# A graph layer's message loop on one core: additions, clipping and bf16 splitting moved into PSUM, two groups at a time

## The chip, the cores and the metric

The kernel runs on one core of one Trainium2 chip. Times are device microseconds of one execution, lower is better. A time shown for a kernel is the median over several executions. The engines are PE (TensorE: matmuls, with PEld for its weight loads), DVE (VectorE), ACT (ScalarE), POOL (GpSimd) and SP (SyncE, which here only issues DMAs). Each works through its own instructions in order and waits on semaphores that others raise.

## The reference

A graph layer with 12500 nodes of 96 features and 412500 edges, which are sorted by their target node. In short:

```python
node_feat = mlp(x, W_node, ...)
edge_feat = mlp(edge_attr, W_edge, ...)          # 4 -> 96
message = concatenate([x[row], x[col], edge_feat], axis=1)
message = mlp(message, W_msg, ...)               # 288 -> 96
agg = segment_sum(message, col, num_segments=N)
x = layernorm(x + agg + node_feat)
```

Here `mlp` is `relu(h @ W + b)`, followed by a normalization of each feature over all rows (all nodes, or all edges). A message's value before its `relu` is therefore the sum of a row of `x @ W_msg[:96]` picked by `row`, a row of `x @ W_msg[96:192]` picked by `col`, and a product of the edge's features. The normalization needs each feature's sum and sum of squares over all edges.

## The kernel before

**Ahead of the loop.** The kernel writes `p_tab` and `q_tab` (the two products of `x`) to HBM, computes the node part and the edge features' statistics (`edge_norm`, L306 to L312), and gathers the rows of `p_tab` for the first 104 groups of edges into HBM (`spill`), through `stage` tiles. A gather (L175) is one indirect DMA, which POOL issues for 128 edges; it fetches 128 rows of 96 floats.

**Groups and blocks.** 128 edges are a tile, 4 tiles a group (`GT`), 4 groups a block (`BG`). There are 806 groups in 202 blocks. 26 blocks ("early") take their rows from `spill` by one DMA into `pb` (L440); the other 176 ("late", 702 groups) take them from tiles `pg`, which POOL fills by four gathers a group, into a ring of `RING` = 21 tiles. The first 21 are gathered ahead of the loop. After that, the gathers of group g + 21 are issued once the addition of group g has read its tile. Early blocks stand among the late ones, about one to seven. The first three early blocks (`RAW`) hold rows of `x` and not of `p_tab`; `convert` multiplies them.

**One step** of the message loop (L568) is one group, k. Its instructions are put in order by hand (`manual_schedule`), so each engine takes them in the order of the source:

- `edges` (L462): PE multiplies the edge features of the next block, all four groups, into `pr`, four banks of PSUM. `prepare` (L469): ACT clips the four into `left`, one instruction of 2048 columns, two steps later.
- `linear` (L475): PE multiplies `left` by `rhs` for group k + 1, four products into one of two banks `z`. `rhs` holds the weights and the 31 rows of `q_tab` that the block's targets lie in; the columns of `left` behind the edge features pick among them.
- `message` (L483): DVE adds `z` (PSUM) and `pg` (SBUF) into `hs` (SBUF). The third one of a block also builds `at`, the 0/1 matrix of edges by target nodes.
- `first_part` (L498), once a block: ACT clips `hs`, copies it to bf16 (`h`, part 0), and squares it into `sq`. `second_part` (L507), a step later: DVE subtracts part 0 from `hs`, ACT copies the rest to bf16 (part 1), DVE sums the squares (L514) and adds them to `squares`. `third_part` (L520): DVE subtracts part 1 and writes part 2. Three bf16 parts carry the fp32 value. These instructions take 1536 columns each.
- `sums` (L525): PE multiplies `at` by the three parts and adds up in `pa`, `LATER` = 6 steps behind. `fold`, `turn` and `add` bring a block's sums into `agg`.

In the last block the three parts are run group by group.

**Order and queues.** SP issues the loads of block s + 2 (`load`, `fetch`) at the start of block s. POOL issues nothing in the loop but gathers.

Of the kernel before, what the change touches and what calls it, by code (L numbers as in the profile page):

```python
# [11 lines left out]
F32 = mybir.dt.float32  # L12
# [41 lines left out]
RING = 21  # L54
RAW = 3
LATER = 6
# [20 lines left out]
def gnn(ctx, tc, t):  # L77
# [265 lines left out]
    def fast(ring):  # L343
# [35 lines left out]
        with tc.tile_pool(name="fix", bufs=1) as fix, tc.tile_pool(name="msg", bufs=2) as work, \  # L379
# [28 lines left out]
            zb = [ps.tile([P, GE], F32, name=f"z{i}", bufs=1) for i in range(2)]  # L408
            nodes_of = zb[0][:, GT * C:GT * C + BG * WN].rearrange("p (k w) -> p k w", w=WN)
            nc.vector.tensor_copy(nodes_of, iota)  # L410

            eas, block, prs, zs, pas, hss, by_node = {}, {}, {}, {}, {}, {}, {}
# [31 lines left out]
            def convert(s):  # L444

                b = order[s]
                px = ps.tile([P, BG, GE], F32, name="pr", bufs=1)
                for i in range(0, BG, 2):
                    for k in range(2 * GT):
                        nc.tensor.transpose(px[:C, k // GT, k % GT * P:(k % GT + 1) * P],  # L450
                                            got[b * BG + i + k // GT][:, k % GT, :], ident)
                    for h in range(2):
                        xt = work.tile([P, BG, GT, C], F32, name="sq", bufs=1)
                        xt = xt.rearrange("p g t c -> p (g t c)")[:C, :GE]
                        nc.scalar.activation(xt, px[:C, h, :], AF.Copy)
                        for k in range(GT):
                            nc.tensor.matmul(px[:, 2 + h, k * C:(k + 1) * C], xt[:, k * P:(k + 1) * P], w_msg[:, 0, :],
                                             start=True, stop=True)
                        nc.vector.tensor_copy(got[b * BG + i + h],
                                              px[:, 2 + h, :GT * C].rearrange("p (k c) -> p k c", c=C))  # L460

            def edges(s):  # L462

                prs[s] = ps.tile([P, BG, GE], F32, name="pr", bufs=1)
                for i in range(min(BG, NG - order[s] * BG)):
                    nc.tensor.matmul(prs[s][:C + WN, i, :], we[Q * i:Q * i + EK + 2, :],  # L466
                                     block[s][Q * i:Q * i + EK + 2, :], start=True, stop=True)

            def prepare(s):  # L469

                n = min(BG, NG - order[s] * BG)
                pr, x = prs[s], left[s % 2]
                nc.scalar.activation(x[:C + WN, :n, :], pr[:C + WN, :n, :], AF.Relu)  # L473

            def linear(k):  # L475
                s, g = steps[k]
                n = min(GT, NT - g * GT)
                zs[k] = zb[k % 2][:, :GT * C].rearrange("p (t c) -> p t c", c=C)
                for i in range(n):
                    nc.tensor.matmul(zs[k][:, i, :], left[s % 2][:KR, g % BG, i * P:(i + 1) * P],  # L480
                                     rhs[:KR, s % RB, g % BG, :], start=True, stop=True)

            def message(k):  # L483
# [3 lines left out]
                z, pg = zs.pop(k), got.pop(g)  # L487
                if i == 0:
                    hss[s] = work.tile([P, BG, GT, C], F32, name="hs")
                nc.vector.tensor_add(hss[s][:, i, :n, :], z[:, :n, :], pg[:, :n, :])  # L490
# [7 lines left out]
            def first_part(s, lo, hi, n):  # L498

                hs, h = hss[s][:, lo:hi, :n, :], hb[s % HB][:, lo:hi, :n, 0, :C]  # L500
                nc.scalar.activation(hs, hs, AF.Relu)  # L501
                nc.scalar.activation(h, hs, AF.Copy)  # L502
                sq = work.tile([P, BG, GT, C], F32, name="sq", bufs=1)
                nc.scalar.activation(sq[:, :hi - lo, :n, :], hs, AF.Square)  # L504
                return sq

            def second_part(s, lo, hi, n, sq, rows=P):  # L507

                hs, h = hss[s][:, lo:hi, :n, :], hb[s % HB][:, lo:hi, :n, :, :]
                nc.vector.tensor_tensor(hs, hs, h[:, :, :, 0, :C], op=OP.subtract)  # L510
                nc.scalar.activation(h[:, :, :, 1, :C], hs, AF.Copy)  # L511
                sum_of = work.tile([P, C], F32, name="sum_of", bufs=1)
                m = n if rows == P else n - 1
                nc.vector.tensor_reduce(sum_of, sq[:, :hi - lo, :m, :].rearrange("p g t c -> p c g t"),  # L514
                                        axis=AX.XY, op=OP.add)
                nc.vector.tensor_add(squares, sum_of, squares)
                if rows < P:
                    nc.vector.tensor_add(squares[:rows], sq[:rows, 0, m, :], squares[:rows])

            def third_part(s, lo, hi, n):  # L520

                hs, h = hss[s][:, lo:hi, :n, :], hb[s % HB][:, lo:hi, :n, :, :]
                nc.vector.tensor_tensor(h[:, :, :, 2, :C], hs, h[:, :, :, 1, :C], op=OP.subtract)  # L523
# [15 lines left out]
            def fold(s):  # L539
                by_node[s] = work.tile([NW, C + 1], F32, name="by_node", bufs=1)  # L540
# [18 lines left out]
            with tc.manual_schedule(engines={ET.SP, ET.Pool, ET.PE, ET.DVE, ET.Activation}):  # L559
# [4 lines left out]
                edges(0)  # L564
                prepare(0)
                linear(0)
                held = {}
                for k in range(len(order) * BG + LATER + 3):  # L568
                    s, g = steps[min(k, n - 1)]
                    whole = s < len(order) - 1  # L570
# [4 lines left out]
                    if k % BG == 1 and k // BG - 1 in held:  # L575
                        del held[k // BG - 1]
                        third_part(k // BG - 1, 0, BG, GT)
                    if k + 1 < n:
                        linear(k + 1)
                    if k < n and g % BG == 3 and s + 1 < len(order) and order[s + 1] < RAW:  # L580
                        convert(s + 1)
                    if k < n:
                        message(k)
                        i, m = g % BG, min(GT, NT - g * GT)
                        if whole and i == BG - 1:
                            held[s] = first_part(s, 0, BG, GT)
                        if i == 0 and s:
                            second_part(s - 1, 0, BG, GT, held[s - 1])
                        if not whole:
                            sq = first_part(s, i, i + 1, m)  # L590
                            second_part(s, i, i + 1, m, sq, min(P, E - (g * GT + m - 1) * P))
                            third_part(s, i, i + 1, m)
                    if k % BG == 2 and 0 <= (k - 10) // BG:
                        fold((k - 10) // BG)
                    if k % BG == 3 and 0 <= (k - 11) // BG:
                        turn((k - 11) // BG)
# [7 lines left out]
                    if k % BG == 0 and 0 <= (k - 12) // BG:  # L604
                        add((k - 12) // BG)
# [243 lines left out]
```

## Time and profile before

| | |
|---|---|
| median of 3 runs | 5155.51 us (5140.26 to 5171.73) |
| the profiled execution | 5138.11 us |
| its span, first to last instruction | 5136.4 us |
| mean granted clock of PE | 0.623 |
| busy: PE, PEld | 2712.5 us (53%), 2042.3 us (40%) |
| busy: DVE, ACT | 2464.7 us (48%), 1912.1 us (37%) |
| busy: POOL | 3475.1 us (68%) |

In a row of groups, "x702 | 379.8, 554 | 1427.8" means 702 instructions, 379.8 us in which one of them ran, 554 ns for one on average, and 1427.8 us in which their engine stood idle just before them; what ended that idle time follows the arrows. "remote" means that a semaphore ended it whose writer the profile can't name, "issue" that no wait is seen. In a row of a time line stand the start and the length in us, then engine, line, operation and tiles, with the idle time before it in brackets. The loop runs from 949 us to 5091 us of the span.

### The profile page before, as it was taken

Reading aid. Unit: us, or ns where it says so; the run is one execution under the profiler, and the core shown is the slowest. Engines: PE = TensorE matmul, PEld = TensorE weight load, DVE = VectorE, ACT = ScalarE, POOL = GpSimd, SP = SyncE. Lnnn points to the kernel's source line nnn. Section 1 sums busy time; section 2 is a strip of 40 time slices with the busy share of each in tenths; the row PEclk is TensorE's granted clock in tenths of the full one; section 3 lists DMA queues with packets and bytes.
Section 4 is the critical chain, followed back from the end, with each engine's and each line's share of the span. In section 5 each row is a group of like instructions: output and inputs, shape, how many; then the busy total and the mean of one; then the engine's idle time right before and its main releaser. Section 6 shows DMA issues by size and latency. Waiting matters only on the chain. (4 is left out here: it accounts for less than half of the span.)

```text
span 5136.4 us, 41113 instructions
## 1 busy us (share of the span) xinstructions
PE 2712.5 (53%) x13498; PEld 2042.3 (40%) x13498; DVE 2464.7 (48%) x3234; ACT 1912.1 (37%) x1413; POOL 3475.1 (68%) x3244
## 2 busy tenths in 40 slices
PE   5566753446455656436546363566446635454465
PEld 3423421344334435325434252455325424343354
DVE  2555753445344546425455362566236525454465
ACT  2244542234234435324334252355224414343343
POOL 6645354276577777767777777777767767777771
PEclk7555555566566657656666575677557656666666
DMA  8433332121122212112112222122212212111222
GB/s 233 118 66 73 72 69 41 25 46 42 29 45 47 46 38 54 41 42 46 44 38 48 44 47 48 37 46 48 47 43 45 47 36 47 43 44 39 45 47 80
DMA packets 190356, 273.95 MB, mean 53 GB/s; under 512 B 121571, under 2 KB 121956, under 8 KB 189126
## 3 DMA queue, kind: packets, MB, share of 16 engines
q0 software_dynamic: 103136, 158.62, 15.4%
q1 hardware_dynamic: 71684, 99.14, 7.0%
q10 hardware_dynamic: 15312, 13.47, 0.9%
q8 instruction: 109, 1.79, 0.2%
q14 instruction: 115, 0.94, 0.1%
HBM read 227.55 MB, written 43.43 MB: 53 GB/s over the span
## 5 line engine op out<-in xcount | busy, mean ns | idle before, releaser
L175 POOL DMA_INDIRECT pg<-p_tab,src x2807 | 3056.7, 1089 | 1210.8 <-issue 785.1
L480 PE MATMUL z<-rhs,left 128*128 128x96 f32 x6446 | 1301.9, 368 | 1737.9 <-DVE hs L490 988.9
L480 PEld LDWEIGHTS z<-rhs,left 128*128 128x128 f32 x6446 | 1205.2, 277 | 2040.9 <-DVE hs L490 1067.3
L490 DVE TENSOR_TENSOR hs<-z,pg 128x384 f32<-128x384 f32 x702 | 379.8, 554 | 1427.8 <-remote 870.7
L535 PE MATMUL pa<-h,at 128*80 128x291 bf16 x3223 | 759.0, 367 | 153.4 <-issue 143.4
L473 ACT ACTIVATE left<-pr 127x2048 f32<-127x2048 f32 x202 | 377.6, 1869 | 911.5 <-remote 825.2
L501 ACT ACTIVATE hs<-hs 128x1536 f32<-128x1536 f32 x203 | 298.9, 1473 | 910.8 <-DVE hs L490 630.2
L175 POOL DMA_INDIRECT stage<-p_tab,src x368 | 354.0, 962 | 321.0 <-DMA spill<-stage 197.6
L514 DVE TENSOR_REDUCE sum_of<-sq 128x96 f32<-128x1536 f32 x203 | 558.6, 2752 | 0.0
L306 PE MATMUL pr<-ea,wide 10*128 10x512 f32 x1212 | 407.6, 1074 | 272.6 <-issue 155.3
L535 PEld LDWEIGHTS <-at 128*80 128x80 bf16 x3223 | 461.3, 153 | 225.0 <-issue 178.3
L511 ACT ACTIVATE h<-hs 128x1536 bf16<-128x1536 f32 x203 | 301.6, 1486 | 656.2 <-DVE hs L510 442.4
L312 DVE BATCH_NORM_STATS2 estats<-r 128x6 f32<-128x512 f32 x606 | 365.9, 678 | 309.2 <-issue 181.1
L510 DVE TENSOR_TENSOR hs<-hs,h 128x1536 f32<-128x1536 f32 x203 | 354.3, 1745 | 305.0 <-issue 201.5
L310 ACT ACTIVATE r<-pr 128x1024 f32<-128x1024 f32 x303 | 295.1, 1024 | 447.7 <-remote 272.0
L306 PEld LDWEIGHTS pr<-ea,wide 10*128 10x128 f32 x1212 | 202.7, 322 | 476.2 <-issue 280.2
L523 DVE TENSOR_TENSOR h<-hs,h 128x1536 bf16<-128x1536 f32 (+1 forms) x203 | 353.0, 1739 | 0.0
L502 ACT ACTIVATE h<-hs 128x1536 bf16<-128x1536 f32 x203 | 302.1, 1488 | 6.5
L504 ACT ACTIVATE sq<-hs 128x1536 f32<-128x1536 f32 x203 | 294.7, 1452 | 0.2 <-DVE sum_of L514 0.2
L466 PE MATMUL pr<-ea,we 7*127 7x512 f32 x1404 | 237.5, 691 | 32.6 <-issue 20.0
L490 DVE TENSOR_TENSOR hs<-z,pb 128x384 f32<-128x384 f32 x104 | 56.5, 554 | 233.6 <-remote 174.3
L494 DVE TENSOR_TENSOR at<-rel,z 128x496 bf16<-128x496 f32 x202 | 134.4, 665 | 63.8 <-remote 44.2
(127 smaller groups left out, 1052.0 us busy)
## 6 DMA issues: line engine op xcount, KB each, us to landing
pg<-p_tab,src POOLq DMA_INDIRECT x2807
spill<-stage SPq DMA_DIRECT2D x26, 768.0 KB
pb<-spill SPq DMA_DIRECT2D x26, 768.0 KB
ea<-in_ea SPq DMA_DIRECT2D x75, 160.0 KB
rhs<-q_tab SPq DMA_DIRECT2D x202, 46.5 KB
ea<-in_ea SPq DMA_DIRECT2D x352, 20.0 KB
stage<-p_tab,src POOLq DMA_INDIRECT x368
y_d<-y0s SPq DMA_DIRECT2D x12, 384.0 KB
```

The lines of the kernel that those rows point to most:

```text
L175: nc.gpsimd.indirect_dma_start(out=pg[:, i, :], out_offset=None, in_=tab[:, :], in_offset=bass.IndirectOffsetOnAxis(ap=idx[:, k:k + 1], ax ...
L306: nc.tensor.matmul(pr[:, k % 2, :], wide[Q * i:Q * i + 2 * EK, :], ea[Q * i:Q * i + 2 * EK, b % J, :], start=True, stop=True)
L312: nc.vector.bn_stats(stats[:, (k - o) % NS, (k - o) // NS, :], r[:, 1 - o, :])
L473: nc.scalar.activation(x[:C + WN, :n, :], pr[:C + WN, :n, :], AF.Relu)
L480: nc.tensor.matmul(zs[k][:, i, :], left[s % 2][:KR, g % BG, i * P:(i + 1) * P], rhs[:KR, s % RB, g % BG, :], start=True, stop=True)
L490: nc.vector.tensor_add(hss[s][:, i, :n, :], z[:, :n, :], pg[:, :n, :])
L502: nc.scalar.activation(h, hs, AF.Copy)
L510: nc.vector.tensor_tensor(hs, hs, h[:, :, :, 0, :C], op=OP.subtract)
L511: nc.scalar.activation(h[:, :, :, 1, :C], hs, AF.Copy)
L514: nc.vector.tensor_reduce(sum_of, sq[:, :hi - lo, :m, :].rearrange("p g t c -> p c g t"), axis=AX.XY, op=OP.add)
L523: nc.vector.tensor_tensor(h[:, :, :, 2, :C], hs, h[:, :, :, 1, :C], op=OP.subtract)
L535: nc.tensor.matmul(pas[s][:NW, :3 * (C + 1)], at[s % HB][:r, i, o + NW * t:o + NW * (t + 1)], h[:r, t, :, :].rearrange("p a c -> p (a c)") ...
```

## The change

The values of a group no longer go to `hs`. DVE adds `pg` to the product where it lies, in PSUM, and clipping, subtracting and splitting work there too. For that `z` becomes two buffers of two banks, each for a pair of groups. The three parts run for each pair, with instructions of 768 columns, and a buffer comes free for the products of the pair after next when the third part has read it. `pr` shrinks from four banks to two, so that `edges` and `prepare` run twice a block, for half of it each. `convert` goes group by group. The space of `hs` and of a smaller `sq` makes a ring of 26 tiles possible. `sums` run 4 steps behind; `fold`, `turn` and `add` follow one step after another.

```diff
-RING = 21
+RING = 26
-LATER = 6
+LATER = 4
...
-            zb = [ps.tile([P, GE], F32, name=f"z{i}", bufs=1) for i in range(2)]
+            zb = [ps.tile([P, 2, GE], F32, name=f"z{i}", bufs=1) for i in range(2)]
...
-            def edges(s):
-
-                prs[s] = ps.tile([P, BG, GE], F32, name="pr", bufs=1)
-                for i in range(min(BG, NG - order[s] * BG)):
-                    nc.tensor.matmul(prs[s][:C + WN, i, :], we[Q * i:Q * i + EK + 2, :],
-                                     block[s][Q * i:Q * i + EK + 2, :], start=True, stop=True)
...
+            def edges(s, half):
+
+                n = min(2, NG - order[s] * BG - 2 * half)
+                if n > 0:
+                    prs[s, half] = ps.tile([P, 2, GE], F32, name="pr", bufs=1)
+                for i in range(n):
+                    o = Q * (2 * half + i)
+                    nc.tensor.matmul(prs[s, half][:C + WN, i, :], we[o:o + EK + 2, :], block[s][o:o + EK + 2, :],
+                                     start=True, stop=True)
...
+                    nc.scalar.activation(x[:C + WN, 2 * half:2 * half + n, :], pr[:C + WN, :n, :], AF.Relu)
...
-                if i == 0:
-                    hss[s] = work.tile([P, BG, GT, C], F32, name="hs")
-                nc.vector.tensor_add(hss[s][:, i, :n, :], z[:, :n, :], pg[:, :n, :])
+                z = zb[k // 2 % 2][:, k % 2, :n * C].rearrange("p (t c) -> p t c", c=C)
+                nc.vector.tensor_add(z, z, got.pop(g)[:, :n, :])
...
+            def parts(k, m, n):
+
+                s, g = steps[k]
+                z = zb[k // 2 % 2][:, k % 2:k % 2 + m, :n * C].rearrange("p g (t c) -> p g t c", c=C)
+                return z, [hb[s % HB][:, g % BG:g % BG + m, :n, a, :C] for a in range(3)]
+
+            def first_part(k, m=2, n=GT):
+
+                z, h = parts(k, m, n)
+                nc.scalar.activation(z, z, AF.Relu)
+                nc.scalar.activation(h[0], z, AF.Copy)
+                sq = work.tile([P, 2, GT, C], F32, name="sq")
+                nc.scalar.activation(sq[:, :m, :n, :], z, AF.Square)
+                return sq
...
+            def second_part(k, sq, m=2, n=GT, rows=P):
+
+                z, h = parts(k, m, n)
+                nc.vector.tensor_tensor(z, z, h[0], op=OP.subtract)
+                nc.scalar.activation(h[1], z, AF.Copy)
+                sum_of = work.tile([P, C], F32, name="sum_of")
...
+            def third_part(k, m=2, n=GT):
+
+                z, h = parts(k, m, n)
+                nc.vector.tensor_tensor(h[2], z, h[1], op=OP.subtract)
...
+                    if k % 2 and 3 <= k <= last + 1:
+                        third_part(k - 3)
                     if k + 1 < n:
                         linear(k + 1)
                     if k < n:
                         message(k)
...
+                    if k % 2 == 0 and 2 <= k <= last:
+                        second_part(k - 2, sq)
+                    if k % 2 and k < last:
+                        sq = first_part(k - 1)
...
                     if 0 <= k - LATER < n:
                         sums(k - LATER)
                     if k < n and s + 1 < len(order):
-                        if g % BG == 0:
-                            edges(s + 1)
-                        if g % BG == 2:
-                            prepare(s + 1)
+                        (prepare if g % 2 else edges)(s + 1, g % BG // 2)
+                        if g % BG == 3 and order[s + 1] < RAW:
+                            convert(s + 1)
```

More of the change, by code (lines that the diff above doesn't have):

```diff
@@ L446, in convert @@
                 b = order[s]
[L447 to L460, printed above, removed]
@@ L462, in edges @@
[L462 to L473 removed]
+                px = ps.tile([P, 2, GE], F32, name="pr", bufs=1)
@@ L563, in fast @@
                 fetch(1)
-                edges(0)
-                prepare(0)
+                for half in range(2):
+                    edges(0, half)
+                    prepare(0, half)
                 linear(0)
-                held = {}
+                sq, last = None, BG * (len(order) - 1)
                 for k in range(len(order) * BG + LATER + 3):
                     s, g = steps[min(k, n - 1)]
-                    whole = s < len(order) - 1
                     if k < n and g % BG == 0:
```

76 lines of the change are left out of this document (33 added, 43 removed).

## The prediction

> **What bounds the kernel now.** I read the groups first, then the waits, then time lines and windows. The page's chain of waits covers only the last 45 us, so the message loop has to be read from the other views. Gathers are POOL's `DMA_INDIRECT` (L175); 2807 of them feed the loop. From the groups by line:
>
> ```profile
> span 5136.4 us, 41113 instructions
> ...
> L175 POOL DMA_INDIRECT pg<-p_tab,src x2807 | 3056.7, 1089 | 1210.8 <-issue 785.1 <-DVE hs L490 379.6 <-DMA pg<-p_tab,src 44.5
> ...
> L514 DVE TENSOR_REDUCE sum_of<-sq 128x96 f32<-128x1536 f32 x203 | 558.6, 2752 | 0.0
> ...
> L490 DVE TENSOR_TENSOR hs<-z,pg 128x384 f32<-128x384 f32 x702 | 379.8, 554 | 1427.8 <-remote 870.7 <-PE z L480 267.7 <-DMA pg<-p_tab,src 117.3
> L473 ACT ACTIVATE left<-pr 127x2048 f32<-127x2048 f32 x202 | 377.6, 1869 | 911.5 <-remote 825.2 <-issue 35.9 <-PE pr L466 23.2
> ...
> L310 ACT ACTIVATE r<-pr 128x1024 f32<-128x1024 f32 x303 | 295.1, 1024 | 447.7 <-remote 272.0 <-issue 114.8 <-PE pr L306 44.8
> ```
>
> POOL's account of these gathers is 3056.7 + 1210.8 = 4267.5 us, about the whole time from its first one (748 us) to its last (5016 us). The reader is to see that DVE's adds hardly wait for gathered rows (117 us), and that 871 us end with "remote", a releaser that the profile can't name. The time lines show what stretches a gather:
>
> ```profile
> 2999.74 1.76 DVE L510 TENSOR_TENSOR hs<-hs,h 128x1536 f32<-128x1536 f32 x1 [2.31 <-ACT sq L504]
> ...
> 3000.78 1.53 POOL L175 DMA_INDIRECT pg<-p_tab,src  x1 [0.30 <-issue]
> ...
> 3004.96 1.75 DVE L523 TENSOR_TENSOR h<-hs,h 128x1536 bf16<-128x1536 f32 x1
> 3005.11 2.41 POOL L175 DMA_INDIRECT pg<-p_tab,src  x1 [0.30 <-issue]
> ...
> 3009.08 0.95 POOL L175 DMA_INDIRECT pg<-p_tab,src  x1 [0.30 <-issue]
> 3009.29 0.56 DVE L490 TENSOR_TENSOR hs<-z,pg 128x384 f32<-128x384 f32 x1 [0.70 <-PE z L480]
> ...
> 3010.33 0.94 POOL L175 DMA_INDIRECT pg<-p_tab,src  x1 [0.30 <-issue]
> ...
> 3014.29 1.76 DVE L510 TENSOR_TENSOR hs<-hs,h 128x1536 f32<-128x1536 f32 x1 [1.81 <-issue]
> ```
>
> A gather takes 0.94 us and one starts every 1.25 us. One that begins inside L523 (both inputs in SBUF) is held until L523 ends, 2.41 us in all; one inside L490 (one input in PSUM) isn't. So (1089 - 944) x 2807 = 407 us of POOL is time held by DVE. A block takes 14.55 us here (2999.74 to 3014.29), while 16 gathers need 20 us. DVE eats faster than POOL supplies, yet the gathers aren't what it waits for. The windows of the edge statistics, ahead of the loop, where DVE has no such operation, tell why:
>
> ```profile
> 728.40:739.40 11.00, 11.00 (x41) 7.78 (x37) 11.00 (x20) 7.90 (x8) 8.50 (x9) 0.50 0.57 104
> 739.40:853.00 113.60, 25.99 (x51) 6.03 (x48) 16.45 (x26) 12.28 (x12) 85.85 (x91) 0.50 0.26 56
> 853.00:867.00 14.00, 2.08 (x4) 0.50 (x4) 1.29 (x2) 1.44 (x2) 0.00 (x0) 0.50 0.02 4
> 867.00:881.00 14.00, 13.29 (x42) 6.99 (x45) 12.52 (x21) 11.53 (x13) 0.00 (x0) 0.50 0.25 36
> ```
>
> The columns after the length are busy time and count of PE, PEld, DVE, ACT and POOL. POOL gathers from 728.45 to 852.97 without a pause. PE keeps its pace for 11 us (41 matmuls), then does 51 in 113.6 us, 0.45 per us, and is back only 15 us after POOL has stopped. The granted clock is 0.50 in all four rows, so it isn't the clock. A shorter run of 19.7 us shows the same with a shorter return:
>
> ```profile
> 709.28 0.94 POOL L175 DMA_INDIRECT stage<-p_tab,src  x1 [0.30 <-issue]
> ...
> 712.80 8.04 PE L306 MATMUL pr<-ea,wide 10*128 10x512 f32 x24 [2.13 <-ACT r L310]
> ...
> 867.66 12.86 PE L306 MATMUL pr<-ea,wide 10*128 10x512 f32 x39 [5.62 <-ACT r L310]
> ```
>
> PE returns 2.6 us after that run (690.57 to 710.22) and 14.7 us after the one of 124.5 us: 12 to 13% of the run. I read it as a backlog that unbroken gathers build up and only a pause drains. What passes between the engines I can't name. In the loop L510 and L523 hold POOL for 0.6 + 1.5 us in 14.55 us, 14%, which is just enough. When a block comes late, they come too rarely, and it tips over:
>
> ```profile
> 2993.00:3022.00 29.00, 18.55 (x115) 15.41 (x115) 19.24 (x25) 15.78 (x11) 22.93 (x20) 0.74 0.19 38
> 2129.00:2245.00 116.00, 24.93 (x83) 16.27 (x84) 19.46 (x24) 11.47 (x8) 79.47 (x81) 0.50 0.17 34
> ...
> 2132.86 0.56 DVE L490 TENSOR_TENSOR hs<-z,pg 128x384 f32<-128x384 f32 x1 [9.59 <-remote]
> ...
> 2233.86 0.56 DVE L490 TENSOR_TENSOR hs<-z,pg 128x384 f32<-128x384 f32 x1 [7.93 <-remote]
> ```
>
> 57 matmuls make a block; 115 in 29 us are two blocks, 83 in 116 us one and a half, and one block's adds take from 2132.86 to 2233.86, 101 us, with POOL gathering at its full pace. It ends when the ring is full and POOL has to wait for an add:
>
> ```profile
> POOL pg L175 <- DVE hs L490: 379.6, 87, 100.9
> ...
> 852.02 0.95 POOL L175 DMA_INDIRECT pg<-p_tab,src  x1 [0.31 <-issue]
> 953.86 0.94 POOL L175 DMA_INDIRECT pg<-p_tab,src  x1 [100.89 <-DVE hs L490]
> ...
> 5091.14 0.14 issue
> ```
>
> So the loop is set by POOL's pace plus the pauses that PE needs. The row of waits is us, times, longest.
>
> **The change part by part.**
>
> Add, subtract and split in PSUM: L510 and L523 lose an SBUF input. 407 us of held gathers go; the only DVE operation with two SBUF inputs left is the 0.26 us add into `squares`, which I cost at nothing since a gather of 3009.08's kind rarely meets it. With that go the two forced breathing spaces per block. No row shows DVE writing PSUM; 0.55 us (L490, PSUM in) is the nearest, bounded by 2752/4 = 0.69 us per 384 columns (L514) and 1.75/4 = 0.44 (L523). Even 0.69 adds 0.14 x 4 = 0.6 us a block, under POOL's 20.
>
> Pairs instead of fours, half blocks for edges: ACT's 1024 columns take 1.024 and 2048 take 1.869, so each extra instruction costs 0.18 us; five more a block are 0.9 us on ACT, and three more big ones with one small add some 0.8 us on DVE. Both engines idle a third of the block (15.78 and 19.24 busy of 29), which hides it; without that cover it would be 202 x 0.9 = 180 us, between 0 and that.
>
> New waits: PE's products of pair e+4 wait for the third part of pair e, with the sums, the edge products and the next product queued behind them. The loop third part, product (2.02 us, below), add 0.55, subtract 0.95, reduce 1.4, squares 0.26, third part 0.95 gives 6.2 us per pair, 12.4 a block, 3.1 per group, shorter than today's 14.55. The sums come two steps earlier with no cost. Edge products wait for ACT's half block, which the third part of the same pair waits for as well. SP's issues stay as they are.
>
> Conversion of three blocks goes group by group: four chains instead of two pairs, 0 to 15 us in all; I take 0 since POOL's pauses there already cover it.
>
> Ring of 26: 20 more gathers, 25 us, fit into the 100.9 us wait ahead of the loop, leaving 2703; the five more groups at the end cost 5 x 3.1 = 15.5 us back.
>
> **The sum.** POOL now runs unbroken until the ring is full. One cycle: PE works for 11 us (728.4 to 739.4; bounds 7.6, the harmless stretch from L523's end to the next L510, and 12), plus some 2 us of the pause: 13/3.1 = 4.2 groups, and 0.2 while starved (8 us x 0.45 / 14 matmuls per group). 702 of 806 groups free a slot, so 4.4 x 0.87 = 3.83 slots x 5.0 us = 19.2 us of gathers. Then POOL pauses: 0.12 x 19.2 = 2.3 for the drain, 1.6 for half of a step of PE (2.02 + 1.18, rows below), and 0.83 from an add's start to the gather, less the usual 0.3.
>
> ```profile
> 3021.80 2.02 PE L480 MATMUL z<-rhs,left 128*128 128x96 f32 x8 [4.63 <-DVE hs L490]
> ...
> 3009.05 1.18 PE L535 MATMUL pa<-h,at 128*80 128x291 bf16 x4
> ...
> 953.03 0.56 DVE L490 TENSOR_TENSOR hs<-z,pg 128x384 f32<-128x384 f32 x1 [17.82 <-PE z L480]
> ```
>
> That is 4.4 us, the cycle 23.6 us for 4.4 groups, 5.36 each. Total: 953 to the first add, 780 x 5.36 = 4181, the last 26 groups x 3.1 = 81, the end 5136.4 - 5091.1 = 45, and 1.7 between span (5136.4) and that run's time (5138.1): 5262 us, 2.4% above the profiled execution. The median of the runs shown, 5155.5, is 17 above it, so I predict 5280. With a pause of only 2.3 us it would be 4890; with 7.6 us of good time (3.3 groups, 14.4 us of gathers) and a pause of 6 us, (14.4 + 6)/3.3 = 6.2 per group, 5900.
>
> The Trainium skill, page "SBUF — State Buffer", section "Who interferes with whom", says that a DVE instruction with at most one SBUF input doesn't contend with GpSimd, that DMA never contends with a compute engine and that PE waits on nobody. The first agrees with L490 beside an unheld gather. By the other two PE would not starve, and the time would be the first rival's; 51 matmuls in 113.6 us speak against it.
>
> **The rivals.**
>
> PE doesn't starve (faster). Place: POOL. 953.9 + 2703 x 1.25 = 4333 to the last gather, some 15 for the last groups, 45 and 2: 4395, up to 4500 with a few full-ring waits. For it: the 407 us, and DVE's block of 12.4 us below POOL's 20. Against it: the windows. It decides if PE keeps its pace beyond 20 us of unbroken gathers.
>
> Balance (faster): starvation sets in softly, POOL is held by exactly the drain, 12%: the 4890 above. For it: each add frees one slot only, so the feedback is prompt. Against it: PE's fall is steep, 41 in 11 us, then 0.45 per us.
>
> PE never recovers in pauses of a few us: a group costs 5.0 + 12 matmuls at 0.25 = 3.0 + 0.6 drain = 8.6, so 676 x 8.6 + 104 x 3.1 = 6136, and 7200 in all. Against it: 2.6 us sufficed after a 19.7 us run.
>
> The lock stays, because DVE takes the shared port for PSUM operands too: as before, within 0.5% of 5155. Against it: L490.
>
> **How the numbers follow.** Forecast 0.53, no starvation 0.17, balance 0.15, no recovery 0.10, lock stays 0.05. 0.5% either side of 5155 (5130 to 5181) is about what a measurement of this kernel can tell. The forecast's own range is 5000 to 5600; 0.05 of it lies below 5130 and 0.02 inside the band. Faster 0.17 + 0.15 + 0.05 = 0.37, same 0.07, slower 0.56. From 4500 to 5800 leaves out most of the first and third rivals, about 0.18.
>
> **What would show it.** Gathers of 0.94 us throughout (mean under 960 ns) show the lock gone; if they stay near 1089, that step fell. Starvation shows as stretches with under one matmul per us while POOL gathers, and as POOL waits for adds above 600 us; rival one as POOL busy over 75% of the loop and adds that wait for gathered rows. Pauses near 2.3 us mean balance. DVE operations in PSUM over 0.69 us per 384 columns would break the costing.

## The result, and the profile after

| | before | after |
|---|---|---|
| time, median of 4 runs in turn (us) | 5147.9 (5138.6 to 5171.7) | 5662.4 (5660.9 to 5669.4) |
| ratio, 95% interval | 1 | 1.099 (1.095 to 1.104) |
| profiled execution: time, span (us) | 5138.1, 5136.4 | 5663.3, 5661.5 |
| gathers, busy and idle ahead of them (us) | 3056.7, 1210.8 | 2654.7, 2051.9 |
| first add, last gather, last add (us) | 953, 5016, 5077 | 990, 5465, 5606 |

Slower, as forecast, but by 10% where the forecast said 2.4. The groups of the changed kernel first (line, engine, operation, tiles, count; busy and mean ns; idle time ahead and what ended it):

```profile
L175 POOL DMA_INDIRECT pg<-p_tab,src x2807 | 2654.7, 946 | 2051.9 <-DVE z L488 1241.6 <-issue 809.7 <-DMA pg<-p_tab,src 0.6
...
L518 DVE TENSOR_REDUCE sum_of<-sq 128x96 f32<-128x768 f32 x404 | 580.2, 1436 | 0.0
...
L488 DVE TENSOR_TENSOR z<-z,pg 128x384 f32<-128x384 f32 x702 | 393.1, 560 | 2148.8 <-remote 989.3 <-PE z L479 713.4 <-PE pr L465 270.6
L514 DVE TENSOR_TENSOR z<-z,h 128x768 f32<-128x768 f32 x404 | 387.5, 959 | 8.6 <-ACT sq L508 1.7
```

A gather takes 946 ns on the mean, where it took 1089: the lock is gone, all 400 us of it, and the operations in PSUM cost what was forecast (560 ns per 384 columns, 959 per 768). POOL gained nothing by it: what it no longer spends inside gathers it spends waiting for adds. The row of waits (us, times, longest):

```profile
POOL pg L175 <- DVE z L488: 1241.6, 176, 102.9
```

In the kernel before it was 379.6 us in 87 waits. The time line of the changed kernel shows of what these waits consist (start, length, engine, line; in brackets the idle time ahead and what ended it):

```profile
990.38 1.17 DVE L488 TENSOR_TENSOR z<-z,pg 128x384 f32<-128x384 f32 x2 [20.63 <-PE z L479]
991.22 0.95 POOL L175 DMA_INDIRECT pg<-p_tab,src  x1 [102.90 <-DVE z L488]
...
3006.05 0.57 DVE L488 TENSOR_TENSOR z<-z,pg 128x384 f32<-128x384 f32 x1 [8.46 <-PE pr L465]
3006.89 0.95 POOL L175 DMA_INDIRECT pg<-p_tab,src  x1 [3.60 <-DVE z L488]
...
3023.28 1.35 PE L479 MATMUL z<-rhs,left 128*128 128x96 f32 x8
...
3025.65 0.95 POOL L175 DMA_INDIRECT pg<-p_tab,src  x1 [0.30 <-issue]
3029.59 0.57 DVE L488 TENSOR_TENSOR z<-z,pb 128x384 f32<-128x384 f32 x1 [8.68 <-remote]
...
3036.87 1.38 PE L479 MATMUL z<-rhs,left 128*128 128x96 f32 x8
...
3038.28 0.57 DVE L488 TENSOR_TENSOR z<-z,pb 128x384 f32<-128x384 f32 x1 [3.92 <-PE z L479]
...
3048.12 0.57 DVE L488 TENSOR_TENSOR z<-z,pg 128x384 f32<-128x384 f32 x1 [4.16 <-PE z L479]
3048.95 0.95 POOL L175 DMA_INDIRECT pg<-p_tab,src  x1 [22.36 <-DVE z L488]
...
3072.35 0.95 POOL L175 DMA_INDIRECT pg<-p_tab,src  x1 [3.69 <-DVE z L488]
```

Three things are to be seen. First, the cycle: POOL gathers without a break from 3006.89 to 3026.60, 16 gathers, one block, and then stands until an add frees a slot. From 3048.95 to 3072.35 it is the same again: 23.4 us a block, the pause 3.6. Second, the block between them adds rows of the spill (`pb`), which frees no slot, and POOL stands for its whole length, 22.4 us. Of the waits over 1 us after the first, 143 are of the short kind (519 us together) and 25 of the long kind (617 us: 22 of 22 to 23 us and three of 41, where rows are converted). Third, PE's late results: the product of 3023.28 ends at 3024.63, and the add that needs it starts 5.0 us later, with POOL gathering until 3026.60. That add waits for PE's semaphore alone, and the trace has it raised three times within 0.1 us, from 3029.56 on. The product of 3036.87, with POOL at rest, ends at 3038.25, and its add starts at once.

PE itself keeps its pace meanwhile. The window of that run of gathers and of the pause behind it (length, then busy time and count of PE, PEld, DVE, ACT and POOL, granted clock, DMA share, GB/s):

```profile
3006.90:3026.60 19.70, 13.46 (x57) 9.95 (x57) 9.25 (x15) 8.08 (x10) 15.12 (x16) 0.57 0.22 47
3026.60:3030.10 3.50, 0.00 (x0) 0.00 (x0) 0.52 (x2) 0.00 (x0) 0.00 (x0) 0.61 0.08 14
```

All 57 matmuls of a block lie inside the run of gathers, none in the pause. No run of gathers in this loop has PE under 1.7 matmuls per us; what is late is the word of the last ones.

The first add comes 37 us later than before, though the wait ahead of the loop was to swallow the 20 extra gathers. The row of a window there shows PE doing 36 matmuls in 107 us beside POOL's gathers:

```profile
781.00:888.00 107.00, 18.69 (x36) 4.52 (x36) 11.58 (x18) 9.22 (x9) 81.03 (x86) 0.50 0.25 51
```

### The profile page after: what moved, and what is told of

Read it like the earlier page. It is cut to its first block, busy times and chain, and to the rows that moved or that the text cites. A ratio compares the mean times of both kernels' runs of the same rounds, so it can differ in the third digit from the quotient of the medians.

```text
span 5661.5 us, 43662 instructions
## 1 busy us (share of the span) xinstructions
PE 3247.9 (57%) x13498; PEld 2389.5 (42%) x13498; DVE 2541.9 (45%) x4038; ACT 1990.8 (35%) x2418; POOL 3073.2 (54%) x3244
## 5 line engine op out<-in xcount | busy, mean ns | idle before, releaser
L175 POOL DMA_INDIRECT pg<-p_tab,src x2807 | 2654.7, 946 | 2051.9 <-DVE z L488 1241.6
L479 PEld LDWEIGHTS z<-rhs,left 128*128 128x128 f32 x6446 | 1430.0, 324 | 2277.6 <-DVE h L527 1635.9
L488 DVE TENSOR_TENSOR z<-z,pg 128x384 f32<-128x384 f32 x702 | 393.1, 560 | 2148.8 <-remote 989.3
L515 ACT ACTIVATE h<-z 128x768 bf16<-128x768 f32 x404 | 329.4, 815 | 1779.6 <-DVE z L514 1606.8
L505 ACT ACTIVATE z<-z 128x768 f32<-128x768 f32 x404 | 320.5, 793 | 1085.2 <-DVE z L488 809.8
L518 DVE TENSOR_REDUCE sum_of<-sq 128x96 f32<-128x768 f32 x404 | 580.2, 1436 | 0.0
L473 ACT ACTIVATE left<-pr 127x1024 f32<-127x1024 f32 x403 | 415.2, 1030 | 75.4 <-remote 28.6
L514 DVE TENSOR_TENSOR z<-z,h 128x768 f32<-128x768 f32 x404 | 387.5, 959 | 8.6 <-ACT sq L508 1.7
L527 DVE TENSOR_TENSOR h<-z,h 128x768 bf16<-128x768 f32 x404 | 382.2, 946 | 0.4
L506 ACT ACTIVATE h<-z 128x768 bf16<-128x768 f32 x404 | 330.5, 818 | 12.8
L508 ACT ACTIVATE sq<-z 128x768 f32<-128x768 f32 x404 | 322.5, 798 | 0.0
```

What stands on the lines that cost most here:

```text
L175: nc.gpsimd.indirect_dma_start(out=pg[:, i, :], out_offset=None, in_=tab[:, :], in_offset=bass.IndirectOffsetOnAxis(ap=idx[:, k:k + 1], ax ...
L473: nc.scalar.activation(x[:C + WN, 2 * half:2 * half + n, :], pr[:C + WN, :n, :], AF.Relu)
L479: nc.tensor.matmul(zb[k // 2 % 2][:, k % 2, i * C:(i + 1) * C], left[s % 2][:KR, g % BG, i * P:(i + 1) * P], rhs[:KR, s % RB, g % BG, :], ...
L488: nc.vector.tensor_add(z, z, got.pop(g)[:, :n, :])
L506: nc.scalar.activation(h[0], z, AF.Copy)
L514: nc.vector.tensor_tensor(z, z, h[0], op=OP.subtract)
```

## The experiments

Theory M: gathers issued back to back make what PE finishes reach the others late, so POOL has to pause; with the ring full, POOL and the consumer (PE, ACT and DVE) run in step, and each early block stops POOL. Rival R1: nothing starves, and the consumer's longer chain sets the pace. Rival R2: a pause of POOL is lost time, whatever it did in the first trials.

Ratios are to the kernel before, run in turn on the same chip; its medians there lie between 5159 and 5295 us, so times of different chips compare only roughly. Kernels that were run once have no interval.

**The consumer alone.** Both kernels, with no gathers in the loop:

```diff
+            kept = [got[g] for g in range(SPILL, SPILL + RING)]
...
-                        got[ahead] = ahead_of(ahead)
+                        got[ahead] = kept[(ahead - SPILL) % RING]
```

> The changed kernel, with no gathers issued inside the message loop: every group takes one of the 26 sets of rows gathered ahead of the loop, so the products are summed over the wrong rows; all the work of PE, ACT and DVE stays. It shows the consumer's own pace. Theory M (unbroken gathers make PE's signals late, POOL and the consumer run in step, and only the blocks that free no slot run at the consumer's own pace): those blocks take 18.5 us each in the changed kernel, so 990 us to the first add + 201 x 18.5 + 45 = about 4750 us. Rival R1 (no starvation; the consumer's longer chain alone sets the pace): still 23 us per block, about 5600 us. As I had costed the chain (12.4 us per block): about 3530 us.

> The kernel before with no gathers inside the loop: every group takes one of the 21 sets of rows gathered ahead of the loop, so the products are summed over the wrong rows. The consumer's own pace before the change. Theory M: 14.55 us per block, the pace of its undisturbed blocks, so 953 + 201 x 14.55 + 45 = about 3920 us, against 19.3 us per block measured for the changed kernel: the change lengthened the consumer's chain by 4 to 5 us a block. Rival R1 (the consumer's chains are alike and the gathers set both): 19 us per block, about 4820 us.

Measured 4906 us for the changed kernel and 4031 for the one before. A window of each, with the adds alone (length, busy time and count of the adds, granted clock, DMA share, GB/s), changed kernel first:

```profile
1400.00:4700.00 3300.00, 393.65 (x703) 0.68 0.04 11
```

```profile
1400.00:3900.00 2500.00, 366.40 (x688) 0.73 0.05 15
```

Four adds make a block: 3300/703 x 4 = 18.8 us, and 14.5 us before. So the change made the consumer 4.3 us a block slower by itself, and with gathers a late block takes 23.4. R1 falls on that gap, and so does my 12.4. Both times are above M's 4750 and 3920: part of it is the three blocks with converted rows, which M had left out (37 us each in the changed kernel).

**Both products of a pair together.** The first add of a pair also waits for the second product, since both lie in one PSUM tile, and PE does its turn and sums between them.

```diff
                 linear(0)
+                linear(1)
...
-                    if k + 1 < n:
-                        linear(k + 1)
+                    if k % 2:
+                        for j in (k + 1, k + 2):
+                            if j < n:
+                                linear(j)
```

> The changed kernel with both products of a pair issued together right behind the third part that frees their bank (linear(k+1) and linear(k+2) at odd k), so that the first add no longer has PE's turn and sums between the two products it waits for. Takes about 2 to 4 us per block out of the consumer's chain. Theory M: the late blocks stay with POOL's cycle of 23.3 us, only the 26 early blocks gain some 4 us: 5540 to 5600 us. Rival R1 (the chain sets the pace): 201 x 2 to 4 us less, 4860 to 5260 us.

Measured 5680 us, 1.075 (1.070 to 1.081). R1's 4860 to 5260 isn't there. The ratio is below 1.099, but the kernel before took 5271 us on this chip and 5148 in the first comparison, and the changed kernel itself wasn't run here; so M's 5540 to 5600 is judged by the trace. POOL's time line has the long stop shorter by under 2 us and the short one no shorter (4.0 us at the median, 3.6 in the changed kernel), which is no gain to speak of:

```profile
1614.44 0.95 POOL L175 DMA_INDIRECT pg<-p_tab,src  x1 [3.91 <-DVE z L488]
1654.83 0.95 POOL L175 DMA_INDIRECT pg<-p_tab,src  x1 [20.68 <-DVE z L488]
```

**The two holds put back,** as work that serves nothing, without and with the pairs:

```diff
-RING = 26
+RING = 25
...
+            spare = fix.tile([P, 96, 16], BF16, name="spare")
...
+                        nc.vector.tensor_tensor(spare, rel[:, :384, :]..., rel[:, 384:768, :]..., op=OP.add)
```

> The changed kernel with the two holds of POOL per block put back as useless work: a DVE operation with two SBUF inputs and 1536 columns after the first part of each pair, into a spare tile (ring of 25 to make room for it). Theory M: a pause spread over the gathers is as good as the pause that comes of a full ring, and the consumer can run ahead of it again, so part of the early blocks hides: 5100 to 5250 us, with POOL's waits for adds under 500 us. Rival R1 (no starvation, DVE and the chain are the bound): DVE's extra 1 to 1.75 us twice a block can only lengthen it, 5660 us or more, up to 201 x 3.5 = 700 us more.

> Both edits: products of a pair together, and the two holds per block, ring of 25. Theory M: the consumer has both its breathing spaces and a chain of 15 to 16 us per block, so early blocks hide in the ring: 4950 to 5080 us, at or below the kernel before. Rival R1: 4860 to 5260 us plus up to 700 us for the extra DVE work, and slower than the paired products alone.

Measured 5500 us, 1.040 (1.034 to 1.047), and 5282 us, 0.997 (0.993 to 1.002). The groups of the first:

```profile
L175 POOL DMA_INDIRECT pg<-p_tab,src x2807 | 3108.0, 1107 | 1423.5 <-issue 739.9 <-DVE z L489 584.9 <-DMA pg<-p_tab,src 93.0
L590 DVE TENSOR_TENSOR spare<-rel 128x1536 bf16<-128x1536 f32 x402 | 702.4, 1747 | 0.0
```

702 us of useless work on DVE, and gathers of 1107 ns again: R1 expects 5660 us or more, and the time is below that. With the shorter chain as well, the kernel is back at the time of the one before. M's direction holds, its sizes (5100 to 5250, and 4950 to 5080 with the pairs) don't: 16 and 6 stops of 12 to 32 us were left. The likely reason, not tested, is that the holds come with the consumer, and come too seldom just when it is late.

**A pause in POOL's own order.** A memset of a spare tile ahead of each group's gathers, in the loop alone (first three; the ring is 25 in all kernels with such pauses in the changed loop):

```diff
+            idle = fix.tile([P, 768], BF16, name="idle")
...
+                        nc.gpsimd.memset(idle, 0.0)
                         got[ahead] = ahead_of(ahead)
```

> The changed kernel with a pause in POOL's own order: a memset of a spare tile (768 columns, some 0.5 to 1.4 us) ahead of each group's four gathers inside the loop, ring of 25 to make room. No engine but POOL does anything more. Theory M (PE's signals fall behind while POOL issues gathers back to back, and a pause of some 12 per cent lets them catch up): POOL's pauses now come evenly, so the consumer runs at its own 18.5 to 19.3 us per block, below POOL's 22 to 23, the ring doesn't fill, and the early blocks hide: about 5000 to 5150 us, faster than the two holds of DVE (5500) and than the kernel before. Rival R2 (what holds gave back came of DVE's own timing, or the gathers' rate doesn't matter): each memset is paid in full, 676 x 0.6 = 400 us on top, 5700 to 6000 us.

> The same pause of POOL, and the two products of a pair issued together. Theory M: consumer at 16 to 17.5 us per block, further below POOL's, so a block that comes late is made good sooner: 4950 to 5100 us, a few per cent below the kernel before. Rival R2: 5700 to 6000 us.

> The same with two memsets per group. Theory M: if one memset is enough for PE, the second only lengthens POOL's cycle by its own time, 676 x 0.5 to 0.9 = 340 to 600 us above the kernel with one; if one is too short and stretches with slow PE remain, the second removes them and gives less than that, or gains. Rival R2: another 400 us on top in any case.

Measured 5652 us (before: 5295), 5560 us, 1.050 (1.043 to 1.057), and 5430 us with two memsets. M's figures for one memset fell, and R2's for one and for two: more pause gave less time. The waits of the kernel with two:

```profile
DVE z L489 <- DMA pg<-p_tab,src: 1481.0, 376, 10.0
...
POOL pg L175 <- DVE z L489: 57.0, 18, 40.4
```

POOL hardly waits for adds (40.4 of the 57 us lie ahead of the loop), and the adds wait for rows: the starvation is over, and the pause is longer than it need be. How long it was I had put wrong. The gap between a group's last gather and the next is 0.92 us with one memset and 1.70 with two, 0.30 without: pauses of 0.62 and 1.40 us per four gathers (5.0 us), 12% and 28%.

**The pauses ahead of the loop.** The same trouble stands in the edge statistics of the kernel before, with no ring, no lock and no add near it. One or two memsets behind every four gathers there, nothing in the loop:

```diff
                 gather(b * BG + i, pg[:, i, :, :])
+                nc.gpsimd.memset(idle, 0.0)
...
-            got = {g: ahead_of(g) for g in range(SPILL, SPILL + RING)}
+            got = {}
+            for g in range(SPILL, SPILL + RING):
+                got[g] = ahead_of(g)
+                nc.gpsimd.memset(idle, 0.0)
```

> The kernel before, with two memsets of a spare tile (about 0.75 us each) in POOL's order behind every four gathers that run ahead of the message loop; the loop itself is as before. A test of the pause where no add, no ring and no lock of DVE plays a part. Theory M: the edge statistics' 1212 matmuls, which need 340 us at their full pace (36 in 10 us) but are spread over 675 us between stretches with 4 in 10 us, are no longer held up, so the first add comes 50 to 100 us earlier and the whole is 1.0 to 2.0 per cent below the kernel before. Rival R2 (pauses are only lost time): POOL's gathers ahead of the loop end some 30 us or more later, first add at the same time or up to 30 us later, 0 to 0.6 per cent above.

> The same with one memset behind every four gathers (a pause of 0.8 us in 5.8). Theory M: in the loop of the changed kernel one memset left part of the slow stretches and two left none, so here too it gives a part of what two give: 0.3 to 1.5 per cent below the kernel before. Rival R2: 0 to 0.3 per cent above.

> The kernel before with one memset behind every four gathers ahead of the loop, the spare tile now kept to the end (ring of 20 to make room), so that no tile of the message loop has to wait for the last memset. Theory M: first add at 770 to 790 us instead of 827, the loop unchanged: 40 to 60 us less than the 5029 us of the earlier trial, 3 to 4 per cent below the kernel before. If the earlier start is lost again behind POOL's pace in the loop: about 5030 us.

Measured 5029 us, 0.985 (0.968 to 1.002), with two; 5029 us, 0.977 (0.960 to 0.994), with one; 4983 us, 0.973 (0.943 to 1.002), with one and the spare tile kept. The windows (PE, PEld, DVE, ACT, POOL) and the time line of the last:

```profile
660.00:710.00 50.00, 41.21 (x88) 12.56 (x88) 27.27 (x43) 21.50 (x21) 40.41 (x45) 0.50 0.29 63
```

```profile
801.60 0.56 DVE L495 TENSOR_TENSOR hs<-z,pg 128x384 f32<-128x384 f32 x1 [17.92 <-PE z L485]
802.43 0.95 POOL L176 DMA_INDIRECT pg<-p_tab,src  x1 [33.08 <-DVE hs L495]
```

While POOL gathers, PE does 88 matmuls in 50 us, 1.8 per us, at a granted clock of 0.50, where it did 0.45 per us at the same clock in the kernel before. The first add comes at 802 us instead of 953 (851 with two memsets, 827 with one). Pauses made the preparation shorter, so R2 falls here. The gain in the whole time is less sure: of the three intervals only the second lies below 1. M's size held for two memsets (1 to 2 per cent). One gave no less than two, where M expected a part, and the last kernel missed its 770 to 790 us and its 3 per cent.

**Both places, and how the loss divides.** The changed kernel with two memsets behind every four gathers ahead of the loop, and inside it none (a_prepace), one of 928 columns (a_pace10), one and a quarter (a_pace12, and with pairs), one and a half (with pairs).

> The changed kernel with the products of a pair together, ring of 25, two memsets behind every four gathers ahead of the loop, and one and a half (1.13 us) ahead of each group's gathers inside it. Theory M: between one memset (5560 us, still 90 waits for adds) and two (5430 us, POOL never stopped) lies the pause that is just enough: 900 to 930 us to the first add, 676 x 6.2 = 4190, the last groups 110, the end 50: 5250 to 5300 us, about the kernel before on these chips. If the pauses only cost time: no better than 5430 to 5560.

> The changed kernel, its product order untouched (consumer 19.1 us per block), with two memsets behind every four gathers ahead of the loop and one and a quarter (0.95 us) ahead of each group's gathers inside it; ring of 25. Theory M: the loss was POOL standing still behind a full ring, so with a pause that is just enough POOL never waits for an add, the early blocks hide, and the long chain costs nothing: 770 us to the first add, then POOL's 676 x 6.05 = 4090 and some 150: 5000 to 5100 us. If the chain of 19.1 us were what costs: 3 per cent or more above the kernel with paired products in the same call.

> The same with the products of a pair together (consumer 17.2 us per block). Theory M: within 1 per cent of the kernel without them, 5000 to 5080 us, 1 to 3 per cent below the kernel before; some 100 us below the kernel with a pause of 1.13 us if 0.95 is still enough, and POOL's waits for adds come back (over 300 us) with 5200 us or more if it isn't.

> The changed kernel with two memsets behind every four gathers ahead of the loop and none inside it, ring of 25. Theory M: first add at 770 us instead of 990 to 1010, and the loop as in the changed kernel: blocks of 23.3 us locked to a full ring, with a stop of POOL of some 22 us in every early block. The whole gain of the earlier start stays, since the loop is in step with the consumer from its start: 5662 - 220 = 5440 us, 5 to 6 per cent above the kernel before; the 300 us from there to the 5138 us of the kernel with pauses in both places are then what the stops inside the loop cost. If the stops weren't the loss: within 1 per cent of 5138 us.

> The changed kernel with pauses in both places, where the pause inside the loop is one memset of 928 columns, about 0.95 us more per four gathers (0.8 was too short, 1.2 enough); ring of 25. If 0.95 is still enough: 676 x 0.25 = 170 us less than 5138, so 4970 to 5010 us, 3 per cent below the kernel before. If it is too short: POOL waits for adds again, over 200 us of it, and 5050 us or more.

| kernel | pause per 4 gathers in the loop (us) | stops of POOL over 12 us: number, us | time (us) | ratio to before |
|---|---|---|---|---|
| the change | none | 25, 617 | 5662 | 1.099 (1.095 to 1.104) |
| a_prepace | none | 24, 581 | 5487 | 1.059 (1.052 to 1.066) |
| a_pace10 | 0.75 | 3, 49 | 5114 | 0.986 (0.980 to 0.993) |
| a_pace12 | 1.21 | none | 5138 | 1.002 (0.998 to 1.006) |
| a_pair_pace12 | 1.21 | none | 5138 | 1.002 (0.998 to 1.005) |
| a_pair_pace15 | 1.21 | none | 5147 | 1.005 (1.000 to 1.009) |

The time line of a_prepace shows an early start and the stops still there; that of a_pace10 what the pause is (0.17 us of issue behind the memset in place of the usual 0.30):

```profile
766.33 1.17 DVE L495 TENSOR_TENSOR z<-z,pg 128x384 f32<-128x384 f32 x2 [20.61 <-PE z L486]
...
1452.16 0.94 POOL L176 DMA_INDIRECT pg<-p_tab,src  x1 [22.89 <-DVE z L495]
1475.73 0.94 POOL L176 DMA_INDIRECT pg<-p_tab,src  x1 [3.17 <-DVE z L495]
```

```profile
3002.49 0.95 POOL L176 DMA_INDIRECT pg<-p_tab,src  x1 [0.31 <-issue]
3003.43 0.89 POOL L615 MEMSET idle<- 128x928 bf16 x1
3004.48 0.95 POOL L176 DMA_INDIRECT pg<-p_tab,src  x1 [0.17 <-issue]
```

One memset a group takes 373 us off the whole (5487 to 5114) and nearly all the long stops with it; R2 falls in the loop too. The adds' waits that end with "remote", which is how PE's late word looks from DVE, go the same way: 1153 us in the changed kernel, 1073 in a_prepace, 318 in a_pace10, none in the three below it and none in the kernels without gathers. The pairs no longer matter: 5138 with and without them, though the chain is 18.8 us long in the one. So with pauses the long chain costs nothing, and what it cost without them came by way of POOL's stops behind a full ring. Sizes of mine were off: a_prepace kept 175 of its 220 us; a_pace12 and its pairs were to stay under 5100 and 5080, with a pause of 0.95 us that came out at 1.21; a_pair_pace15, put at 5250 to 5300, took 5147. And a_pace10 was to give under 5010 if its pause was enough: with 5114 and 160 us of waits for adds left, 0.75 us (15%) is nearly enough. In the three kernels listed below it the gap comes out at 1.52 us, whether the second memset has 192 or 384 columns, so a pause between 0.75 and 1.21 wasn't tried.

**What the pause is owed to.** Fewer instructions on PE, or fewer bytes in a gather:

```diff
-                for t in range(n):
+                for t in range(1 if i == 0 else 0):
...
```

```diff
-                        got[ahead] = ahead_of(ahead)
+                        got[ahead] = gather(ahead, kept[(ahead - SPILL) % RING], C // 2)
```

> The changed kernel with the products of a pair together, and without the sums over nodes (15 of 16 of these matmuls and their weight loads are left out, so the output lacks them): 57 matmuls and loads per block become about 42. The sums no longer lie in the chain of the pair in either kernel. It asks what sets the pause that a late block needs. If PE's own number of instructions does (each has to be signalled, and they pile up): pause per block down by a quarter, late block 22.6 us instead of 23.7, blocks without gathers 18 us instead of 20.7, about 5400 to 5450 us. If the gathers' number alone sets it (a share of their time, 12 to 18 per cent, whatever PE does): late block still 23.5 to 23.7 us, 5600 to 5680 us.

> The changed kernel with gathers inside the loop that bring 48 of the 96 columns of a row (as many gathers and rows, half the bytes), into the 26 sets of rows that were gathered ahead; the sums are of wrong rows. If the backlog comes with the number of gathers: run of 19.8 us and pause of 3.6 us as before, 5600 to 5700 us. If it comes with the bytes: pause of about 2 us, late block 21.5 us, 5250 to 5400 us. If a gather itself is much shorter with half a row, POOL's run shrinks with it, and the pause as a share of the run tells.

Measured 5558 and 5662 us. POOL's time line without the sums, then with half the bytes:

```profile
1623.21 0.95 POOL L175 DMA_INDIRECT pg<-p_tab,src  x1 [20.75 <-DVE z L488]
1646.40 0.95 POOL L175 DMA_INDIRECT pg<-p_tab,src  x1 [3.48 <-DVE z L488]
```

```profile
1635.43 0.94 POOL L175 DMA_INDIRECT pg<-p_tab,src  x1 [22.40 <-DVE z L488]
1658.83 0.94 POOL L175 DMA_INDIRECT pg<-p_tab,src  x1 [3.74 <-DVE z L488]
```

Half the bytes change nothing: 5661.6 against 5662.4 us, the same stops, the same 0.94 us. So it isn't the bytes. Whether it is the number of gathers or of the rows they fetch stays open, since this kernel keeps both. A quarter fewer matmuls shorten the late block from 23.7 us (a_pair) to 23.2, where the count of PE's instructions as the cause asked for 22.6, and the gathers alone for no less than 23.5. The time, 5558, lies between the two forecasts as well; it comes from another chip and with a granted clock of 0.52 in place of 0.60. PE's count isn't the main cause, but how large its part is this run doesn't tell.

## Why the prediction was right in kind and wrong in size

**The lock** went, as said: 946 ns a gather, no gain from it. **PE's results came late**, as said, and POOL stood for it: waits for adds above 600 us were the sign named, and they are 1242. The other sign, stretches with under one matmul per us while POOL gathers, is there ahead of the loop (36 in 107 us) and not inside it. **The costs in PSUM** and the added instructions lie where they were put, beside other work. ("No row shows DVE writing PSUM" overlooked L410, a copy of 124 columns in 0.29 us; nothing hung on it.) The rivals fall: consumers do wait for PE's late results, the pauses aren't 2.3 us, PE recovers in 3.6, the lock doesn't stay.

**The cycle's length is partly luck:** 23.6 us forecast (19.2 of gathers, 4.4 of pause), 23.4 measured (19.7 and 3.6). The forecast let PE work for 11 us, at 3.1 us a group. Measured, PE works through the whole run of gathers, at 4.7 us a group (18.8 a block), and one late result closes the block. With 4.7 in place of 3.1 the same working gives 13/4.7 + 0.2 = 3.0 groups and a cycle of some 16.6 us.

**The step that failed** is the one that turned the cycle into a time: "702 of 806 groups free a slot, so 4.4 x 0.87 = 3.83 slots". It spreads the groups that free no slot evenly over the cycles, as if they could pass while POOL gathers. But they come as whole blocks of four, and with the ring full there is nothing for POOL to gather while one passes: a cycle holds one late block, and each early block comes on top with the consumer's full 18.8 us. So the pauses, forecast as 2703/15.3 = 177 of 4.4 us, 778 us, became 143 of 3.6 and 25 long ones, 1136 us. That the ring was to be full at every such block was said in the forecast itself ("POOL now runs unbroken until the ring is full"); the next question, what a block does that frees nothing, wasn't asked.

**The consumer's chain** failed with it, and is the larger part of the size: 12.4 us a block for 18.8. I put one product (2.02 us) into the pair's loop. The bank's tile holds two, the add waits for both, and the turn, the sums and the second product pass in between. This made the last groups 60 us dearer and sets the length of each long stop (18.8 and a pause of 3.6 are its 22.4); it does not set the late block, which stayed at 23.7 us with the shorter chain of the pairs. The conversions, put at 0 since pauses were to cover them, added some 18 us to each of three long stops.

By terms of the span (5661.5 against 5260.3 in the sum): the loop up to the last gather took 4473.6 us in place of 4181, +293; the last groups behind it 141.5 in place of 81, +60; the start +37; the rest +10. By estimate, 25 x (18.8 - 12.4) = 160 of the 293 are the chain's, 55 the conversions', and some 80 are left for the even spread. Without the long stops the chain's 160 would have stayed hidden behind POOL, as it does in a_pace12.

**The ring of 26** was to swallow 25 us of gathers ahead of the loop. Those gathers run while the edge statistics do, and hold up PE by my own mechanism: they ended at 888 us instead of 853, and the wait for the first add behind them was as long as before (102.9 us, 100.9 before). So the first add came 37 us later. I had applied the mechanism to the loop and not to the part of the program where I had read it off.

**The sign** was right, and no run shows a gain hidden in the change: a_pace10, at 0.986 (0.980 to 0.993), has nearly no stops and the pauses ahead of the loop as well, and such pauses alone brought the kernel before to between 0.973 and 0.985. On one chip, though not in turn, it took 4983 us and a_pace10 5114. The kernel before with pauses inside its loop wasn't run.

## What to carry to other kernels

When a wait or a lock is taken away, look for what it gave time to: here two locked DVE operations a block were a pause in which PE's results got through (put back as useless work, they took time off), and POOL's gathers, freed of them, stopped for longer at the ring. Where a ring's producer and consumer run in step, ask of every kind of block what it frees, since one that frees nothing stops the producer for its whole length. A producer off the critical path can be too fast: a memset of 0.9 us ahead of every four gathers took 373 us off this kernel, once the gathers ahead of the loop had pauses too.

## What the runs showed of the hardware

What I hadn't expected is how the starvation looks from PE's side. The time line of the kernel before, inside its long run of gathers:

```profile
746.47 2.08 PE L306 MATMUL pr<-ea,wide 10*128 10x512 f32 x4 [2.83 <-ACT r L310]
...
770.62 1.02 ACT L310 ACTIVATE r<-pr 128x1024 f32<-128x1024 f32 x1 [10.18 <-remote]
...
771.68 1.28 DVE L312 BATCH_NORM_STATS2 estats<-r 128x6 f32<-128x512 f32 x2 [9.91 <-issue]
...
771.70 2.08 PE L306 MATMUL pr<-ea,wide 10*128 10x512 f32 x4 [9.12 <-issue]
...
781.82 1.02 ACT L310 ACTIVATE r<-pr 128x1024 f32<-128x1024 f32 x1 [10.18 <-remote]
...
816.18 1.02 ACT L310 ACTIVATE r<-pr 128x1024 f32<-128x1024 f32 x1 [10.93 <-remote]
```

DVE and PE start within 0.1 us of ACT's end (771.64), so ACT's signals arrive at once. PE's come late, and by more than the 5 us seen in the loop. `pr` has four buffers, and PE is four steps ahead of ACT: the four matmuls that it starts at 771.70, in the buffer that ACT has just freed, are those that ACT's step of 816.18 needs (counted off: 1212 matmuls and 303 steps of ACT, four to one). They end at 773.78, by the profile's model of their ends, 42 us before that step. Those that ACT's step of 781.82 needs started at 746.47 and ended 33 us before it; ahead of the run of gathers this lag was under 1 us. So PE isn't short of work, what it has done isn't known: it runs on until its four buffers are used up, which is part of the 11 us for which it kept its pace. Then a step comes through every 11.2 us, nine gathers, and the pause behind the run works off the steps that are owed.

In the loop a pause of 12% of the gathers' time was too little against it, 15% nearly enough, 24% plenty; the bytes of a gather don't matter. Whether the signal is late or the matmul itself no record here tells, and through what a gather holds it up stays open.
